# A graph attention layer on one core: edge values by four 64x64 products, the messages' weights through PSUM, the clip in two parts

## The chip, the core and the metric

The program runs on one core of one Trainium2 chip. The metric is device microseconds from launch to end; lower is better. Three runs of the kernel before gave 1743.85, 1745.33 and 1745.64 us.

## The reference

A layer of graph attention over N = 6250 nodes of 64 values (4 heads of 16) and 206250 edges, sorted by destination, and then a sum with x and a layer norm of each node:

```python
Qh = (x @ Wq.T + bq).reshape(n, H, D)          # Kh, Vh alike
Ee = (edge_attr @ We.T + be).reshape(-1, H, D)
score = (Kh[src] * Qh[dst] * (1.0 / np.sqrt(D)) * Ee).sum(-1)
score = jnp.exp(jnp.clip(score, -5.0, 5.0))
msg = Vh[src] * score[..., None]
wV = jax.ops.segment_sum(msg, dst, num_segments=n)
x = _layernorm(x + wV.reshape(n, H * D), axis=-1)
```

## The kernel before

After a first part that makes tables of K, V and Q for all nodes, the edges are worked through in 202 groups g of 8 tiles of 128 edges. A loop over g holds one step of each stage of a software pipeline, and the order in which a step's instructions are written is the order in which each engine runs them. Waits between engines are set by the framework from what each instruction reads and writes.

The stages of one group, with the engine and the line of each:

- edges(g), on TensorE: the 64x64 matrix We times the edge attributes of 1024 edges, in f32. The attributes come as a tile of 128 partitions, where partitions 0 to 63 hold the 64 attributes of the even tiles of edges and partitions 64 to 127 those of the odd ones. We stands twice in a 128x128 matrix with zeros beside (we_sb), and one product of 128 by 512 fills the PSUM bank ee. It runs three groups ahead.
- biased(g), on ScalarE (L695): adds the bias, ee to eb in SBUF.
- queries(g), on TensorE: picks the rows of Q that the edges need, by a one-hot matrix. These are two products with 64 output rows each, one to partitions 0 to 63 and one to partitions 64 to 127 of the bank qq.
- terms(g), on VectorE (L708): eb times qq. turn(g), on TensorE (L713): four f32 transposes of the result into the bank qe.
- products(g), on VectorE: K of the sources times qe (L732), a sum over each head's 16 values (L735), and the clip to -5 and 5 (L737). weigh(g), on ScalarE (L741): the exponential, in place in SBUF. message(g), on VectorE (L753): V times the weight, into qe.
- keep and take (L765, L770), on ScalarE and VectorE: split the f32 message into three bf16 parts.
- sums(s), on TensorE: for a pair s of groups, 16 products of 192 columns that add the messages of each destination, into the 192 columns pa of the bank room. add(s), on VectorE (L805, L811): adds the three parts into sum_, the last 64 columns of the same bank, and then into the nodes' accumulators.

Beside this runs a second stream. Of every group some of the K and V rows aren't fetched from the table but picked on TensorE: VectorE makes one-hot blocks (hots, L644), five and then three or four blocks in a step, and for each block TensorE runs three products of 512 columns (picks, the tiles pick0 and pick1). These picks are the body of each step on TensorE. About every third group a batch of picks ends; then a product with the bias (bkv_p) and eight f32 products (w2, x) make K and V of it. The other K and V rows are gathered by GpSimd (L260), which issues each gather at a marked place in TensorE's order.

On TensorE a step is written as: edges(g+3), the picks (in every second step with four of the 16 sums after each two blocks but the first two), turn(g+1), queries(g+2), and the sums that are left. All of these products are recorded at one line, L684, so they are told apart by tile. On VectorE add(s) is written near the step's end, ahead of terms(g+2).

## Time and profile before

| | |
|---|---|
| median of three runs | 1745.33 us |
| the profiled execution | 1744.26 us |
| its span, first to last instruction | 1742.4 us |
| TensorE busy | 95% of the span |
| VectorE busy | 90% |
| GpSimd busy | 75% |
| ScalarE busy | 53% |
| granted TensorE clock, mean | 0.974 |

The span is what the trace covers; 1.9 us of the execution lie around it. Busy time says how long an engine had an instruction in work. Matmuls overlap each other in the records, so the length of one matmul's record is not what it costs TensorE: the cost is the time from its start to the start of the next one, called its slot below.

### The profile page before, as it was taken

Reading aid. Unit: us, or ns where it says so; the run is one execution under the profiler, and the core shown is the slowest. Engines: PE = TensorE matmul, PEld = TensorE weight load, DVE = VectorE, ACT = ScalarE, POOL = GpSimd, SP = SyncE. Lnnn points to the kernel's source line nnn. Section 1 sums busy time; section 2 is a strip of 40 time slices with the busy share of each in tenths; the row PEclk is TensorE's granted clock in tenths of the full one; section 3 lists DMA queues with packets and bytes.
Section 4 is the critical chain, followed back from the end, with each engine's and each line's share of the span. In section 5 each row is a group of like instructions: output and inputs, shape, how many; then the busy total and the mean of one; then the engine's idle time right before and its main releaser. Section 6 shows DMA issues by size and latency. Waiting matters only on the chain.

```text
span 1742.4 us, 26109 instructions
## 1 busy us (share of the span) xinstructions
PE 1661.7 (95%) x8456; PEld 881.2 (51%) x8611; DVE 1569.6 (90%) x2637; ACT 918.4 (53%) x1507; POOL 1310.5 (75%) x1374
## 2 busy tenths in 40 slices
PE   7779999999999999999999999999999999999964
PEld 6435555555555555555555555555555555555533
DVE  5689999999999999999999999999999999999976
ACT  3655555545555555555555555555555555555553
POOL 7777777777777777777777777777777777777775
PEclk9879999999999999999999999999999999999985
DMA  6744444343443443434434344344343443434331
GB/s 191 246 120 133 112 118 116 102 121 101 117 120 103 120 113 104 122 108 121 121 102 120 104 114 118 99 120 117 106 132 97 120 113 103 121 107 125 108 89 47
DMA packets 115144, 203.65 MB, mean 117 GB/s; under 512 B 55475, under 2 KB 56223, under 8 KB 114885
## 3 DMA queue, kind: packets, MB, share of 16 engines
q1 hardware_dynamic: 70914, 112.68, 21.7%
q0 software_dynamic: 43648, 88.17, 19.5%
q10 hardware_dynamic: 436, 1.04, 0.3%
q8 instruction: 69, 1.13, 0.3%
q14 instruction: 77, 0.63, 0.1%
HBM read 194.18 MB, written 7.59 MB: 116 GB/s over the span
## 4 chain that ended last, share of the span: by engine, by line
PE 90%; DMA 3%; DVE 2%; issue 2%; ACT 2%; POOL 1%; SPq 0%; POOLq 0%; DVEq 0%; ACTq 0%
PE pick L684 62%; PE ee L684 11%; PE room L684 7%; PE qe L713 5%; PE qq L684 4%; DMA kv<-kv_tab,src_i 2%; POOL kv L260 1%; PE ps L462 1%; DMA wkv<-in_wT 1%; DMA et<-in_eT 0%; PE pv L542 0%; DVE score L735 0%; DVE prod L732 0%; DVE term L708 0%; ACT eb L695 0%
## 5 line engine op out<-in xcount | busy, mean ns | idle before, releaser
L260 POOL DMA_INDIRECT kv<-kv_tab,src_i x1324 | 1270.7, 960 | 403.5 <-issue 197.1
L684 PE MATMUL pick<-hot,parts 128*128 128x512 bf16 x4495 | 1052.4, 379 | 8.3 <-issue 0.2
L684 PEld LDWEIGHTS <-parts 128*128 128x128 bf16 x4650 | 451.9, 98 | 527.1 <-issue 73.3
L644 DVE TENSOR_TENSOR hot<-from,still 128x2560 bf16<-128x2560 bf16 x366 | 460.0, 1257 | 0.0
L741 ACT ACTIVATE score<-score 128x32 f32<-128x32 f32 x202 | 46.3, 229 | 732.7 <-DVE score L737 732.7
L765 ACT ACTIVATE msg<-qe 128x512 bf16<-128x512 f32 x400 | 238.6, 596 | 35.8 <-DVE qe L753 26.9
L684 PE MATMUL ee<-et,we_sb 128*128 128x512 f32 x404 | 227.4, 645 | 7.1 <-ACT eb L695 6.1
L249 ACT ACTIVATE to<-to,one_p 126x1024 bf16<-126x1024 bf16 x198 | 226.5, 1144 | 0.0
L243 ACT ACTIVATE to<-kb,minus_row 126x1024 bf16<-126x1024 uint8 x198 | 224.6, 1134 | 0.0
L684 PE MATMUL room<-msg,of 128*128 128x192 bf16 x1592 | 200.2, 252 | 17.6 <-DVE y L811 11.3
L684 PEld LDWEIGHTS <-of 128*128 128x128 bf16 x1600 | 142.8, 100 | 109.5 <-DVE y L811 19.9
L770 DVE TENSOR_TENSOR msg<-qe,msg 128x512 bf16<-128x512 f32 x200 | 136.9, 685 | 67.4 <-ACT msg L765 61.3
L708 DVE TENSOR_TENSOR term<-eb,qq 128x512 f32<-128x512 f32 x202 | 137.0, 678 | 20.1 <-PE qq L684 15.8
L770 DVE TENSOR_TENSOR qe<-qe,msg 128x512 f32<-128x512 f32 x200 | 138.2, 691 | 18.2 <-ACT msg L765 18.2
L732 DVE TENSOR_TENSOR prod<-kv,qe 128x512 f32<-128x512 f32 x202 | 137.3, 680 | 8.2 <-DMA kv<-kv_tab,src_i 3.4
L735 DVE TENSOR_REDUCE score<-prod 128x32 f32<-128x512 f32 x202 | 138.3, 685 | 7.0
L713 PE MATMUL qe<-ident,term 128*128 128x128 f32 x806 | 126.2, 281 | 18.7 <-DVE term L708 18.7
L753 DVE TENSOR_TENSOR qe<-kv,score 128x512 f32<-128x512 f32 x200 | 139.0, 695 | 4.1 <-ACT score L741 4.1
L695 ACT ACTIVATE eb<-ee,be_col 128x512 f32<-128x512 f32 x202 | 135.1, 669 | 4.6 <-PE ee L684 4.6
L724 DVE TENSOR_TENSOR of<-still,key 128x2048 bf16<-128x2048 bf16 (+2 forms) x105 | 122.7, 1169 | 0.2
L713 PEld LDWEIGHTS qe<-ident,term 128*128 128x128 f32 x806 | 97.3, 144 | 49.8 <-DVE term L708 29.9
L684 PE MATMUL qq<-to,qw 126*64 126x512 bf16 x396 | 82.4, 413 | 0.0
(138 smaller groups left out, 855.5 us busy)
## 6 DMA issues: line engine op xcount, KB each, us to landing
et<-in_eT SPq DMA_DIRECT2D x100, 512.0 KB
kb<-key_tab SPq DMA_DIRECT2D x101, 252.0 KB
kv<-kv_tab,src_i POOLq DMA_INDIRECT x1324
srcs<-in_src_rows SPq DMA_DIRECT2D x62, 256.0 KB
qw<-q_tab SPq DMA_DIRECT2D x202, 15.8 KB
kv_tab<-kv_sb SPq DMA_DIRECT2D x4, 640.0 KB
q_tab<-q SPq DMA_DIRECT2D x5, 480.0 KB
y<-in_x_blocks SPq DMA_DIRECT2D x2, 512.0 KB
```

The lines of the kernel that those rows point to most:

```text
L243: nc.scalar.activation(TO[g][:, :n, :], KB.pop(g)[:, :n * P].rearrange("p (j e) -> p j e", j=n), AF.Square, bias=minus_row3[:3 * W])
L249: nc.scalar.activation(TO[g][:, :n, :], TO[g][:, :n, :], AF.Relu, bias=one_p[:3 * W], scale=-1.0)
L260: return nc.gpsimd.indirect_dma_start(out=kv_of(g)[:, j, :], out_offset=None, in_=kv_tab[:, :], in_offset=bass.IndirectOffsetOnAxis(ap=src ...
L644: nc.vector.tensor_tensor(HOT[k][:, :hi - lo].rearrange("p b (a c) -> p b a c", c=2), pairs(FROM[m])[:, None].to_broadcast(shape), block2[ ...
L684: mark.append(nc.tensor.matmul(*aps, **kw))
L708: nc.vector.tensor_mul(TERM[g][:, :n], EB.pop(g)[:, :n], qq[:, :n])
L713: nc.tensor.transpose(qe[g % 2][:, 2 * u:2 * u + 2, :].rearrange("p j c -> p (j c)"), TERM[g][:, u, :], ident)
L732: nc.vector.tensor_mul(prod[:, :n, :], kv_of(g)[:, :n, :C], qe[g % 2][:, :n, :])
L735: nc.vector.tensor_reduce(score, prod[:, :n, :].rearrange("p g (h d) -> p g h d", h=H), axis=AX.X, op=OP.add)
L753: nc.vector.tensor_mul(to.rearrange("p g (h d) -> p g h d", h=H), kv_of(g)[:, :n, C:].rearrange("p g (h d) -> p g h d", h=H), SCORE[g][:, ...
L765: nc.scalar.activation(part, left, AF.Copy)
L770: nc.vector.tensor_sub(left if i == 0 else part_of(g, 2)[1], left, part)
```

## The change

It has four parts.

1. The product of 128x128 by 512 becomes four products of 64x64 by 256 columns. Product (u, r) takes the attributes at partitions 64r to 64r+63 and the matrix We that stands at the same partitions, and writes partitions 64u to 64u+63 of bank r of the tile room, which now has two banks. The halves u are the first and the second half of the group's tiles of edges, so queries and turn index their tiles anew.
2. The tile room holds edge values in columns 0 to 255 of both banks. Bank 0 has pa and sum_ behind them, bank 1 the weights of three groups. The bank of ee is gone, and the count of banks stays at eight.
3. The clip at L737 goes. ScalarE computes relu(5 - score) and then exp(5 - that), which is exp(min(score, 5)), and writes this to PSUM. The message becomes one VectorE instruction that takes the maximum of the weight and exp(-5) and multiplies it with V.
4. The sums of a pair stand in one run of 16 at the end of the step, behind queries, and no more among the picks. add(s) is always written ahead of the picks' part of the step, so on VectorE it comes earlier.

```diff
-            room = fixed.tile([P, 4 * P], F32, name="room")
-            pa = room[:, :3 * C]
-            sum_ = room[:, 3 * C:4 * C]
+            room = fixed.tile([P, 2, 4 * P], F32, name="room")
+            ee = room[:, :, :2 * P].rearrange("p r (i e) -> p r i e", e=P)
+            pa = room[:, 0, 2 * P:2 * P + 3 * C]
+            sum_ = room[:, 0, 2 * P + 3 * C:2 * P + 4 * C]
+            weights = [room[:, 1, 2 * P + C + k * G * H:2 * P + C + (k + 1) * G * H]
+                       .rearrange("p (g h) -> p g h", g=G) for k in range(3)]
...
             def edges(g):
-                n = tiles_of(g) // 2
-                product(ee[:, :n, :], we_sb, ET[g][:, :n, :], start=True, stop=True)
+                n = tiles_of(g) // 4
+                for u in range(2):
+                    for r in range(2):
+                        rows = slice(r * C, (r + 1) * C)
+                        product(ee[u * C:(u + 1) * C, r, :n, :], we_sb[rows, rows],
+                                ET[g][rows, u * n:(u + 1) * n, :], start=True, stop=True)
...
-                nc.vector.tensor_scalar(score, score, -5.0, 5.0, op0=OP.max, op1=OP.min)
...
             def weigh(g):
-                score = SCORE[g][:, :tiles_of(g)]
-                nc.scalar.activation(score, score, AF.Exp)
+                n = tiles_of(g)
+                score = SCORE.pop(g)[:, :n]
+                nc.scalar.activation(score, score, AF.Relu, bias=five_p, scale=-1.0)
+                WEIGHT[g] = weights[g % 3][:, :n]
+                nc.scalar.activation(WEIGHT[g], score, AF.Exp, bias=five_p, scale=-1.0)
...
-                nc.vector.tensor_mul(to.rearrange("p g (h d) -> p g h d", h=H),
-                                     kv_of(g)[:, :n, C:].rearrange("p g (h d) -> p g h d", h=H),
-                                     SCORE[g][:, :n, :, None].to_broadcast([P, n, H, D]))
+                nc.vector.scalar_tensor_tensor(
+                    to.rearrange("p g (h d) -> p g h d", h=H),
+                    WEIGHT.pop(g)[:, :, :, None].to_broadcast([P, n, H, D]), LEAST,
+                    kv_of(g)[:, :n, C:].rearrange("p g (h d) -> p g h d", h=H),
+                    op0=OP.max, op1=OP.mult)
...
-                if g > groups_of(ONES - 1)[-1]:
-                    for s in done:
-                        add(s)
+                for s in done:
+                    add(s)
...
-                summed = 0
-                for i, some in enumerate(by_two(todo)):
+                for some in by_two(todo):
                     picks(some)
-                    if i and parted and g - 1 in ends:
-                        sums(ends[g - 1], summed, summed + 4)
-                        summed += 4
...
                 if g - 1 in ends and now:
-                    sums(ends[g - 1], summed)
+                    sums(ends[g - 1])
...
-                if g <= groups_of(ONES - 1)[-1]:
-                    for s in done:
-                        add(s)
```

How TensorE's order changes at the turn of one step to the next, half way through the program, in the kernel before (the last number of a row counts equal rows; the size is that of the output):

```order
L713 MATMUL qe_759<-ident,term 128x128 x4
L684 LDWEIGHTS qw
L684 MATMUL qq<-to,qw 64x512
L684 LDWEIGHTS qw
L684 MATMUL qq<-to,qw 64x512
L684 MATMUL ee<-et,we_sb 128x512
L684 LDWEIGHTS ones_b
L684 MATMUL pick_753<-bkv_p,ones_b 128x512
```

And at the same place of the kernel after, where lines are numbered anew:

```order
L727 MATMUL qe_760<-ident,term 128x2x64 x4
L691 LDWEIGHTS qw
L691 MATMUL qq<-to,qw 64x512
L691 LDWEIGHTS qw
L691 MATMUL qq<-to,qw 64x512
L691 MATMUL room<-et,we_sb 64x256 x4
L691 LDWEIGHTS ones_b
L691 MATMUL pick_755<-bkv_p,ones_b 128x512
```

One row for the edge values has become four, of half the rows and half the columns each, at the same place between the queries and the next step's products.

On ScalarE a step from its exponential on, before:

```order
L741 ACTIVATE score<-score 128x32
L695 ACTIVATE eb<-ee,be_col 128x512
L243 ACTIVATE to<-kb,minus_row_84 126x1024
L765 ACTIVATE msg<-qe_759 128x8x64
L249 ACTIVATE to<-to,one_p 126x1024
```

and after:

```order
L754 ACTIVATE score<-score,five_p 128x32
L756 ACTIVATE room<-score,five_p 128x32
L706 ACTIVATE eb<-room,be_col 128x2x2x128
L247 ACTIVATE to<-kb,minus_row_84 126x1024
L782 ACTIVATE msg<-qe_761 128x8x64
L253 ACTIVATE to<-to,one_p 126x1024
```

One instruction has come in ahead of the exponential, whose output is now in the tile room, and eb reads that same tile.

On VectorE a step with an add, from the reduction of the scores on, before:

```order
L735 TENSOR_REDUCE score<-prod 128x32
L737 TENSOR_SCALAR score<-score 128x32
L644 TENSOR_TENSOR hot<-from,still 128x2560
L753 TENSOR_TENSOR qe_760<-kv_67,score 128x512
L644 TENSOR_TENSOR hot<-from,still 128x2048
L770 TENSOR_TENSOR qe_760<-qe_760,msg 128x512
L724 TENSOR_TENSOR of<-still,key 128x2048
L770 TENSOR_TENSOR msg<-qe_760,msg 128x8x64
L805 TENSOR_REDUCE room<-room 128x64
L811 TENSOR_SCALAR y<-room,above,y 128x64
L811 TENSOR_SCALAR y<-room,below,y 128x64
L708 TENSOR_TENSOR term<-eb,qq 128x512
```

and after:

```order
L748 TENSOR_REDUCE score<-prod 128x32
L651 TENSOR_TENSOR hot<-from,still 128x2560
L768 TENSOR_SCALAR qe_761<-room,kv_67 128x512
L651 TENSOR_TENSOR hot<-from,still 128x2048
L787 TENSOR_TENSOR qe_761<-qe_761,msg 128x512
L822 TENSOR_REDUCE room<-room 128x64
L828 TENSOR_SCALAR y<-room,above,y 128x64
L828 TENSOR_SCALAR y<-room,below,y 128x64
L737 TENSOR_TENSOR of<-still,key 128x2048
L787 TENSOR_TENSOR msg<-qe_761,msg 128x8x64
L721 TENSOR_TENSOR term<-eb,qq 128x512
```

The clip is gone, the message reads the tile room, and the three instructions of add stand ahead of the one-hot block of the sums (the output named of) instead of behind it.

The framework keeps engines apart by whole PSUM banks. So in the built program the exponential waits for the four edge products of its step, the message waits for eb of its step, and edges(g+3) waits for the last add, the last eb and the last message, since these touch the two banks of room.

More of the change, by code (lines that the diff above doesn't have):

```diff
@@ L1 @@
+import math
 from contextlib import ExitStack
@@ L50 @@
 REST = N - BIG * P
+CLIP = 5.0
+LEAST = math.exp(-CLIP)
 def tiles_of(g):
@@ L602, in tile_gnn @@
                 tc.tile_pool(name="psum", bufs=1, space=bass.MemoryType.PSUM) as psum:
-            OH, OF, EB, TERM, MSG, SCORE, HOT = ({} for _ in range(7))
+            OH, OF, EB, TERM, MSG, SCORE, WEIGHT, HOT = ({} for _ in range(8))
             still = fixed.tile([P, 4 * P], F32, name="still")
@@ L694, in biased @@
                 EB[g] = work.tile([P, G // 2, P], F32, name="eb")
-                nc.scalar.activation(EB[g][:, :n], ee[:, :n], AF.Identity, bias=be_col)
+                nc.scalar.activation(EB[g][:, :n].rearrange("p (i r) e -> p r i e", r=2),
+                                     ee[:, :, :n // 2], AF.Identity, bias=be_col)
             def queries(g):
@@ L700, in queries @@
                 for u in range(2):
-                    product(qq[u * C:(u + 1) * C, :n // 2, :], QW[g], TO[g][:, u:n:2, :],
+                    product(qq[u * C:(u + 1) * C, :n // 2, :], QW[g],
+                                     TO[g][:, u * n // 2:(u + 1) * n // 2, :],
                                      start=True, stop=True)
@@ L710, in turn @@
             def turn(g):
-                for u in range(tiles_of(g) // 2):
-                    nc.tensor.transpose(qe[g % 2][:, 2 * u:2 * u + 2, :].rearrange("p j c -> p (j c)"),
-                                        TERM[g][:, u, :], ident)
+                half = tiles_of(g) // 2
+                for k in range(half):
+                    nc.tensor.transpose(qe[g % 2][:, k:k + half + 1:half, :], TERM[g][:, k, :], ident)
             def onehot_edges(s):
@@ L778, in pa_of, with sums @@
             def pa_of(s):
-                return {NS - 3: px[0][:, :3 * C], NS - 2: px[1][:, :C], NS - 1: ee[:, 0, :C]}.get(s, pa)
-            def sums(s, lo=0, hi=2 * G):
+                return {NS - 3: px[0][:, :3 * C], NS - 2: px[1][:, :C], NS - 1: room[:, 1, 2 * P:2 * P + C]}.get(s, pa)
+            def sums(s):
                 n = tiles_in(s)
-                for j in range(lo, min(hi, n)):
+                for j in range(n):
                     product(pa_of(s), (OF if s >= WHOLE else OH)[s][:, j, :],
```

3 lines of the change are left out of this document (2 added, 1 removed).

## The prediction, as it stood before the changed kernel was run

> **What bounds the kernel now.** I read the page's shares and chain first, then busy time by stage, then TensorE's waits, then its timeline over one step and a half.
>
> ```profile
> span 1742.4 us, 26109 instructions
> PE 1661.7 (95%) x8456; PEld 881.2 (51%) x8611; DVE 1569.6 (90%) x2637; ACT 918.4 (53%) x1507; POOL 1310.5 (75%) x1374
> PE 90%; DMA 3%; DVE 2%; issue 2%; ACT 2%; POOL 1%; SPq 0%; POOLq 0%; DVEq 0%; ACTq 0%
> ```
>
> ```profile
> 0.00:100.00 100.00, 71.37 (x227) 52.92 (x227) 61.76 (x173) 52.72 (x129) 73.78 (x85) 0.89 0.68 205
> 500.00:1000.00 500.00, 497.38 (x2593) 257.79 (x2642) 466.15 (x754) 265.75 (x423) 379.92 (x395) 1.00 0.41 113
> 1690.00:1742.40 52.40, 24.53 (x106) 16.69 (x104) 35.83 (x89) 20.61 (x35) 30.02 (x32) 0.57 0.19 48
> ```
>
> The columns of a stretch are its length, then busy time of PE, PEld, DVE, ACT and POOL. In the middle TensorE is busy 497 of 500 us at full clock; only the first 100 us and the last 52 leave it idle. What TensorE waited for from 100 to 1690 us is this:
>
> ```profile
> PE qe L713 <- DVE term L708: 11.0, 5, 4.6
> PE ee L684 <- ACT eb L695: 3.9, 3, 1.6
> PE pick L684 <- DVE x L666: 1.8, 1, 1.8
> ```
>
> Under 17 us in 1590, and 9 waits in all. So between 100 and 1690 us the time is the sum of TensorE's slots, and a change there counts in full, while VectorE, ScalarE and GpSimd have room. The number of groups in this stretch is that of the clips, 192:
>
> ```profile
> 100.00:1690.00 1590.00, 38.97 (x192) 0.99 0.41 114
> ```
>
> **What a slot costs.** TensorE's timeline over one step and its ends, and three answers of narrower windows that show single starts:
>
> ```profile
> 906.26 0.49 PE L684 MATMUL room<-msg,of 128*128 128x192 bf16 x4
> 906.59 0.60 PE L713 MATMUL qe<-ident,term 128*128 128x128 f32 x4
> 907.12 0.41 PE L684 MATMUL qq<-to,qw 126*64 126x512 bf16 x2
> 907.46 0.50 PE L684 MATMUL room<-msg,of 128*128 128x192 bf16 x4
> 907.80 1.05 PE L684 MATMUL ee<-et,we_sb 128*128 128x512 f32 x2
> 908.69 5.34 PE L684 MATMUL pick<-hot,parts 128*128 128x512 bf16 x24
> 913.87 0.60 PE L713 MATMUL qe<-ident,term 128*128 128x128 f32 x4
> 914.40 0.41 PE L684 MATMUL qq<-to,qw 126*64 126x512 bf16 x2
> 914.74 1.12 PE L684 MATMUL ee<-et,we_sb 128*128 128x512 f32 x2
> 915.70 0.81 PE L684 MATMUL pick<-hot,parts 128*128 128x512 bf16 x2
> ```
>
> ```profile
> 906.70 0.49 PE L713 MATMUL qe<-ident,term 128*128 128x128 f32 x3
> ```
>
> ```profile
> 908.26 0.59 PE L684 MATMUL ee<-et,we_sb 128*128 128x512 f32 x1
> ```
>
> ```profile
> 915.27 0.59 PE L684 MATMUL ee<-et,we_sb 128*128 128x512 f32 x1
> ```
>
> - A pick of 512 bf16 columns: (913.87 - 908.69) / 24 = 0.216 us. A product of sums: 0.33 / 4 = 0.082.
> - One f32 edge product is two matmuls, which I call passes. Each has a slot of 0.43 (915.27 to 915.70, and 908.26 to 908.69), twice a pick's.
> - The first pass's slot is 0.53 behind the queries (914.74 to 915.27) and 0.46 behind sums (907.80 to 908.26). The 0.10 over 0.43 is the loading of f32 weights that nothing hid; behind sums most of it was hidden.
> - The two queries use different halves of the array's columns and take 0.34 together (914.40 to 914.74), 0.12 more than one product of that length. So they run side by side.
> - A change of the array's shape costs: the last transpose ahead of the queries has 0.20 (four take 0.53, and 906.59 to 906.70 is one of 0.11), so 0.09 on the way in. On the way out it is the 0.12, of which 0.05 may be 64 columns of weights, so 0.07.
>
> A group's edge product thus costs 0.96 behind queries, 0.89 behind sums. By the order two of three stand behind queries: 0.94.
>
> **The change on TensorE.** It puts four products in place of one. Each has a quarter of the work and still two passes, 256 columns each: 0.215 (half of 0.43). That makes eight passes, 1.72 us of streaming, and the whole question is how many lie beside each other. The order of issue is first pass, second pass of product (0,0), then both of (0,1), (1,0), (1,1). Two rows bound it: the queries show that neighbours in different parts of the array overlap; the edge product's own passes show that a second pass doesn't start before the first has streamed. If issue is in order, as all starts in the timeline are, the second pass of a product holds up all behind it, and only the next product's first pass joins it. Eight passes then take five rounds, not two. Weights of 64 columns I estimate at 0.05, half of 0.10; the first is bare, and those of the next three products' first passes are issued behind the second pass ahead of them, another 0.05 each. With 0.08 for leaving the shape:
>
> 0.05 + 5 x 0.215 + 3 x 0.05 + 0.08 = 1.355 us, against 0.94: +0.415 us a group, x 192 = **+80 us**.
>
> Two smaller terms. In half the groups the four now stand behind 16 sums in the full array, so they pay 0.09 to enter: 96 x 0.09 = +9. The 62 groups with a bias product behind them paid for that product's own shape already, which the exit now covers:
>
> ```profile
> 898.06 1.12 PE L684 MATMUL ee<-et,we_sb 128*128 128x512 f32 x2
> 899.11 0.39 PE L684 MATMUL pick<-bkv_p,ones_b 3*128 3x512 bf16 x1
> ```
>
> There 1.05 stands for 0.96, so 62 x 0.09 = -6. Sum: +83 us. The ten other groups stand in the start and the tail, where TensorE idles: nothing.
>
> The unknown prices from both sides: if all later weights load hidden, -0.15 x 192 = -29; with loads of 0.10 instead of 0.05, four of them, +38.
>
> **The other engines.** One step without sums on VectorE and ScalarE:
>
> ```profile
> 907.57 0.69 DVE L708 TENSOR_TENSOR term<-eb,qq 128x512 f32<-128x512 f32 x1 [0.60 <-PE qq L684]
> 908.18 0.68 DVE L732 TENSOR_TENSOR prod<-kv,qe 128x512 f32<-128x512 f32 x1
> 908.89 0.69 DVE L735 TENSOR_REDUCE score<-prod 128x32 f32<-128x512 f32 x1
> 909.62 0.18 DVE L737 TENSOR_SCALAR score<-score 128x32 f32<-128x32 f32 x1
> 909.71 1.48 DVE L644 TENSOR_TENSOR hot<-from,still 128x2560 bf16<-128x2560 bf16 x1
> 911.11 0.69 DVE L753 TENSOR_TENSOR qe<-kv,score 128x512 f32<-128x512 f32 x1
> ```
>
> ```profile
> 909.83 0.23 ACT L741 ACTIVATE score<-score 128x32 f32<-128x32 f32 x1 [3.58 <-DVE score L737]
> 909.97 0.67 ACT L695 ACTIVATE eb<-ee,be_col 128x512 f32<-128x512 f32 x1
> ```
>
> Without the clip the one-hot block can start some 0.20 earlier: it stands 0.82 behind the reduction now (908.89 to 909.71), where two neighbours of that length stand 0.61 apart (907.57 to 908.18). The message with two operations isn't in the trace; the nearest row, the same kind on 128x512, takes 0.74 against 0.69 to 0.70:
>
> ```profile
> L666 DVE SCALAR_TENSOR_TENSOR x<-odd,upper,pick 128x512 f32<-128x512 int32 x61 | 44.9, 736 | 0.0
> L753 DVE TENSOR_TENSOR qe<-kv,score 128x512 f32<-128x512 f32 x200 | 139.0, 695 | 4.1 <-ACT score L741 4.1
> ```
>
> So VectorE gains 0.16 a group, worth nothing while TensorE sets the time. ScalarE gets 0.23 a group more, at 53% busy.
>
> New waits: the message now waits for eb as well, since both touch one bank. The reduction ends at 909.58, and ScalarE follows VectorE by 0.03 (the clip ends at 909.80): relu 909.61 to 909.84, exponential 909.87 to 910.10, eb 910.13 to 910.80. The one-hot block of 1.48, from 909.5, covers this. In steps that follow sums, 16 of them from 907.46 end at 908.77, and the four products 1.45 later at 910.22. The exponential waits for them, 0.35 past its 909.87, and the message starts at 911.2 and not 910.9: 0.3 us on VectorE in every second step. Behind the message wait the second one-hot block, the splitting and the terms, which TensorE needs a step later; the 34 us of every 500 that VectorE idles cover it. If that cover went (a TensorE faster than VectorE), it would cost 96 x 0.3 = 29 us. The sums in one run keep their 16 slots of 0.082; add stands earlier, so that the next edges don't wait for it: nothing. The gathers hang on places in TensorE's order and move with it.
>
> **The Trainium skill on this.** "TensorE: Matmul & The Clock Gate", Part 3, section "The mechanism", says that matmuls start and end strictly in program order; by that rule the sum is the 1.355 above, and every start in the timeline agrees. Against it stands "TensorEngine Tiling (Array Packing)", section "Key Properties": tiles work independently, and different ones load and multiply in parallel. By this rule alone the eight passes are two rounds, the first rival's time; the queries agree for one pass each, and no run here shows it for two.
>
> **Rivals.**
> - All four side by side (faster). If a second pass waits at its own part of the array and lets the next product past, a group costs 0.05 + 2 x 0.215 + 0.08 = 0.56: -0.38 x 192 + 3 = -70 us, 1674; with 0.3 us of VectorE's new wait laid bare in part, up to 1700. For it: the queries' overlap. Against it: the second edge pass is never recorded ahead of the first one's end. It decides below four rounds of 0.215: four with their loads cost about as much as today's 0.94.
> - Halves. If only products on the same rows queue behind each other, there are three rounds: 0.05 + 0.645 + 0.05 + 0.08 = 0.825, -0.115 x 192 + 3 = -19 us: 1725.
> - It doesn't do what it says: f32 passes don't overlap at all. Eight rounds and 0.13: 1.85, +0.91 x 192 + 3 = +178 us, 1922. Against it the queries speak, though those are bf16.
>
> **How the numbers follow.** The profiled execution took 1744.26 us, 1.1 below the median shown; 1744 + 83 = **1827 us**. The likeliest case's own range, by the bounds of weights, is 1790 to 1868. Chances: in order 0.60, side by side 0.22, halves 0.07, no overlap 0.07, else 0.04. The range reaches down to side by side and leaves out the 1922: 1674 to 1868. About 0.2% is what a measurement of this kernel can tell from none. Faster by more than that: 0.22 + 0.07 + 0.01 = 0.30; within it 0.03; slower 0.60 + 0.07 = 0.67.
>
> **What would show it.** In the timeline after, the slot from the first edge matmul to whatever follows the four: 1.3 to 1.4 with six or so distinct starts says in order; 0.6 says side by side; 1.8 says no overlap. The picks must keep 0.216 and TensorE 99% busy in the middle; a TensorE that idles for VectorE would prove the cover wrong. VectorE's busy share should fall in the slower cases only because the span grows. I am wrong if the records show second passes starting ahead of the first one's end.

## The result and the profile after

The kernel after took 1728.72 us, the median of four runs from 1727.84 to 1729.15; the kernel before 1744.92. The ratio is 0.9906, with a 95% interval from 0.9894 to 0.9919: 16 us faster, where 83 us slower was forecast.

The page and the stretches of the kernel after, in the views that were shown of before:

```profile
span 1726.9 us, 28900 instructions
PE 1605.5 (93%) x9637; PEld 860.0 (50%) x9823; DVE 1547.7 (90%) x2436; ACT 994.1 (58%) x1709; POOL 1293.2 (75%) x1374
PE 60%; DVE 14%; DMA 8%; ACT 8%; issue 6%; POOL 2%; DVEq 0%; POOLq 0%; SPq 0%; ACTq 0%
```

```profile
0.00:100.00 100.00, 69.06 (x269) 52.63 (x269) 60.29 (x169) 53.99 (x131) 72.91 (x84) 0.86 0.67 205
500.00:1000.00 500.00, 488.75 (x3007) 255.35 (x3066) 470.31 (x710) 292.06 (x490) 378.11 (x401) 1.00 0.42 114
1690.00:1726.90 36.90, 15.04 (x76) 11.24 (x73) 19.90 (x49) 8.66 (x18) 17.75 (x19) 0.55 0.18 45
```

TensorE had 90% of the chain that ended last and has 60% now. VectorE, ScalarE and the gathers' DMAs share 30%. In the middle TensorE idles 11 of 500 us, where it idled under 3. Its waits from 100 to 1690 us:

```profile
PE room L691 <- DVE y L828: 24.8, 17, 6.3
PE room L691 <- DVE acc L828: 10.3, 4, 4.7
PE room L691 <- DVE qe L768: 10.2, 6, 2.5
PE room L691 <- ACT msg L782: 8.0, 3, 4.0
PE qe L727 <- DVE term L721: 3.2, 3, 1.1
```

So 56 us of waits stand where the kernel before had 17, and nearly all of them are of the tile room, in which edge values, sums and weights now live together. TensorE's timeline at the place that the prediction quoted, with an answer of a window that ends 0.04 us behind the first edge product:

```profile
899.30 0.41 PE L691 MATMUL qq<-to,qw 126*64 126x512 bf16 x2
899.64 0.66 PE L691 MATMUL room<-et,we_sb 64*64 64x256 f32 x8
900.23 6.00 PE L691 MATMUL pick<-hot,parts 128*128 128x512 bf16 x26
908.36 0.66 PE L691 MATMUL room<-et,we_sb 64*64 64x256 f32 x8
908.96 0.38 PE L691 MATMUL pick<-bkv_p,ones_b 3*128 3x512 bf16 x1
```

```profile
899.64 0.45 PE L691 MATMUL room<-et,we_sb 64*64 64x256 f32 x4
```

All eight passes have a slot of 0.59 to 0.60 us together (899.64 to 900.23, 908.36 to 908.96), not 1.355. The second answer shows how: four of the eight start at 899.64. In the trace's records they start at 899.636, .643, .649 and .656, and the other four at 899.903, .909, .916 and .923. That is two rounds. If first and second pass of each product are issued one behind the other, as the prediction had it, the second pass of (0,0) waited at its own part of the array and let three products past. The records don't name the product that a pass belongs to; e7 below shows that products do pass each other.

Where TensorE's time went is a sum of slots. I added the time from each matmul's start to the next one's, by tile, from the use of group 12's gathered rows to that of group 186's (174 groups), in us. f1 and k2 are runs of the next section.

| tiles | before | after | f1 | k2 |
|---|---|---|---|---|
| edge products | 168.7 | 104.5 | 103.5 | 103.5 |
| queries | 58.7 | 84.1 | 80.8 | 65.3 |
| sums, picks, batches | 1130.2 | 1140.4 | 1141.9 | 1140.8 |
| transposes | 92.2 | 92.2 | 92.2 | 92.2 |
| the stretch | 1449.8 | 1421.3 | 1418.2 | 1401.8 |

The edge products gave 64 us. Of these, 25 came back in the slots of the queries: the edge products stand behind the queries in half the steps, and their wait for room is counted in the slot ahead of them (22 us; the other 4 are sums that wait for room). Another 10 came back in sums, picks and batches: the last sum's slot ahead of the small products is 0.176, where it was 0.082, as forecast, in 87 of the steps (8 us). So the stretch is 28.5 us shorter; the start and the tail then took 13 us more (what lies behind group 186 is 133.5 us, 123.1 before). This is the second half of the riddle: what made the tail longer, and what TensorE waits for.

### The profile page after: what moved, and what is told of

The parts are those of the page before. It is cut to its first block, busy times and chain, and to the rows that moved or that the text cites. A ratio compares the mean times of both kernels' runs of the same rounds, so it can differ in the third digit from the quotient of the medians.

```text
span 1726.9 us, 28900 instructions
## 1 busy us (share of the span) xinstructions
PE 1605.5 (93%) x9637; PEld 860.0 (50%) x9823; DVE 1547.7 (90%) x2436; ACT 994.1 (58%) x1709; POOL 1293.2 (75%) x1374
## 4 chain that ended last, share of the span: by engine, by line
PE 60%; DVE 14%; DMA 8%; ACT 8%; issue 6%; POOL 2%; DVEq 0%; POOLq 0%; SPq 0%; ACTq 0%
PE pick L691 44%; PE room L691 10%; DMA kv<-kv_tab,src_i 7%; PE qe L727 3%; POOL kv L264 2%; PE qq L691 2%; DVE score L748 2%; ACT eb L706 2%; DVE prod L745 2%; DVE term L721 2%; DVE hot L651 2%; DVE qe L787 1%; DVE qe L768 1%; ACT msg L782 1%; ACT to L253 1%
## 5 line engine op out<-in xcount | busy, mean ns | idle before, releaser
L264 POOL DMA_INDIRECT kv<-kv_tab,src_i x1324 | 1253.4, 947 | 404.7 <-issue 192.6
L691 PE MATMUL pick<-hot,parts 128*128 128x512 bf16 x4464 | 1026.1, 381 | 10.2 <-issue 0.5
L691 PEld LDWEIGHTS <-parts 128*128 128x128 bf16 x4650 | 446.3, 98 | 559.3 <-issue 57.1
L754 ACT ACTIVATE score<-score,five_p 128x32 f32<-128x32 f32 x202 | 64.9, 321 | 661.1 <-DVE score L748 661.1
L691 PE MATMUL room<-msg,of 128*128 128x192 bf16 x1592 | 156.0, 253 | 34.0 <-DVE y L828 14.4
L691 PE MATMUL room<-et,we_sb 64*64 64x256 f32 (+1 forms) x1616 | 139.8, 417 | 37.5 <-DVE y L828 18.4
L768 DVE SCALAR_TENSOR_TENSOR qe<-room,kv 128x512 f32<-128x512 f32 x200 | 139.9, 700 | 31.5 <-ACT eb L706 23.8
L691 PEld LDWEIGHTS <-of 128*128 128x128 bf16 x1600 | 132.8, 100 | 59.6 <-issue 34.5
L706 ACT ACTIVATE eb<-room,be_col 128x512 f32<-128x512 f32 x202 | 138.7, 686 | 9.6 <-PE room L691 1.8
L737 DVE TENSOR_TENSOR of<-still,key 128x2048 bf16<-128x2048 bf16 (+2 forms) x105 | 123.0, 1172 | 0.2
L691 PEld LDWEIGHTS room<-et,we_sb 64*64 64x64 f32 x1616 | 44.0, 136 | 79.1 <-issue 33.0
```

What stands on the lines that cost most here:

```text
L264: return nc.gpsimd.indirect_dma_start(out=kv_of(g)[:, j, :], out_offset=None, in_=kv_tab[:, :], in_offset=bass.IndirectOffsetOnAxis(ap=src ...
L691: mark.append(nc.tensor.matmul(*aps, **kw))
L706: nc.scalar.activation(EB[g][:, :n].rearrange("p (i r) e -> p r i e", r=2), ee[:, :, :n // 2], AF.Identity, bias=be_col)
```

## The experiments

Four theories were tried. A: the gain is lost where edges and sums wait for room. B: VectorE is full. C: the message waits for eb, since ScalarE's new operations stand ahead of it on one tile. D: GpSimd's gathers are a stream that is full, and they end the program. All kernels are the kernel after with an edit, if nothing else is said.

**e1_four_alone** takes the weights out of PSUM again, with the clip of before; the four products and the new order stay.

```diff
+                nc.vector.tensor_scalar(score, score, -5.0, 5.0, op0=OP.max, op1=OP.min)
...
-                nc.scalar.activation(score, score, AF.Relu, bias=five_p, scale=-1.0)
-                WEIGHT[g] = weights[g % 3][:, :n]
-                nc.scalar.activation(WEIGHT[g], score, AF.Exp, bias=five_p, scale=-1.0)
+                nc.scalar.activation(score, score, AF.Exp)
...
+                nc.vector.tensor_mul(to.rearrange("p g (h d) -> p g h d", h=H),
```

> The kernel after with only its first, second and fourth part: four edge products in the shared tile room, but the clip on VectorE, the exponential in SBUF and the message as before. Theory A (TensorE's edge slot fell by 0.34 us a group, 62 us between 120 and 1640 us, and about two thirds came back as waits of the edges for add and of the sums for the message, plus some 8 us in the tail): the message no longer reads room, so the sums wait less, but VectorE has the clip again, 0.2 us a group; 1725 to 1740 us, edge slot 0.60. Rival B (VectorE, 94% busy in the middle, is simply full, and any saving beyond its time is lost): the clip's 0.16 us a group comes on top of the 1729 in full, +31: 1755 or more, no gain over the kernel before. Rival C (the new path of the weights, with the message waiting for eb, costs what was lost): 1690 to 1705.

1740.07 us, 0.9978 (0.9969 to 0.9988). Four products without the weights' path bring 4 of the 16 us. Why the weights help was open at this point; e4 answers it.

**e2_full_array** keeps all but the four products: two products of the full array, 256 columns each.

```diff
-                for u in range(2):
-                    for r in range(2):
-                        rows = slice(r * C, (r + 1) * C)
-                        product(ee[u * C:(u + 1) * C, r, :n, :], we_sb[rows, rows],
-                                ET[g][rows, u * n:(u + 1) * n, :], start=True, stop=True)
+                for r in range(2):
+                    product(ee[:, r, :n, :], we_sb, ET[g][:, r * n:(r + 1) * n, :], start=True, stop=True)
```

> The kernel after, but the edge values by two products in the full 128x128 array, 256 columns each, into the same two banks; all else stays. Four passes of 0.215 with weights loaded twice: an edge slot of 0.95 to 1.1 in place of 0.60. Theory A: TensorE gets 0.35 to 0.5 us a group longer, 67 to 96 us, and the waits for add and message fall by some 30: 1765 to 1795. Rival B (VectorE sets the time): under 1750, since TensorE's 62 us were not what counted. Rival C: like A, less nothing: 1790 or more.

1754.39 us, 1.0063 (1.0047 to 1.008), in none of the three ranges. In its middle TensorE is full again:

```profile
500.00:1000.00 500.00, 496.22 (x2708) 280.90 (x2756) 460.31 (x693) 287.36 (x484) 377.94 (x401) 1.00 0.41 114
```

```profile
903.41 1.13 PE L691 MATMUL room<-et,we_sb 128*128 128x256 f32 x4
904.47 0.39 PE L691 MATMUL pick<-bkv_p,ones_b 3*128 3x512 bf16 x1
```

A slot of 1.06 against 0.60. So the 64x64 products do give the time, 26 us between this kernel and the one after, and the rest of the change costs 9 us by itself.

**e3_add_early** writes add(s) directly behind the products, against the waits for add.

```diff
                     weigh(g)
+                for s in done:
+                    add(s)
...
-                for s in done:
-                    add(s)
```

> The kernel after with add(s) written directly behind the scores' reduction, ahead of the one-hot blocks and the message, so that VectorE does it some 4 us earlier in its step. Theory A: the edges' waits for add, 24 us between 120 and 1640 us, go; VectorE gets no work less. 1700 to 1715, TensorE's waits for add below 6 us. Rival B: the time lost moves to another wait of TensorE for VectorE, 1724 to 1732. Rival C: 1724 to 1732.

1784.89 us, 1.0233 (1.0216 to 1.025): a miss. The waits moved into the chain of every second step, as its waits from 100 to 1690 us show:

```profile
ACT eb L706 <- DVE y L828: 79.3, 79, 1.0
DVE room L822 <- ACT room L756: 66.9, 94, 0.7
```

The second line says that add's first operation, on bank 0, waits for the exponential into bank 1. So the framework keeps engines apart by the whole tile of two banks, not by single banks as the section on the change has it.

**e4_weights_sbuf** lets the exponential write to SBUF, so that the message waits no more for eb.

```diff
-                WEIGHT[g] = weights[g % 3][:, :n]
+                WEIGHT[g] = work.tile([P, G, H], F32, name="weight", bufs=3)[:, :n]
```

> The kernel after with the exponential's output in SBUF in place of room's second bank; relu, exponential and the two-operation message stay. So the message waits for the exponential alone and not for eb, and the exponential not for the edge products. Theory A: VectorE loses 24 us of idle time ahead of the message, so add comes earlier and the edges wait less: 1710 to 1722. Rival B: the same by 24 us less of VectorE's time, 1705 to 1715. Rival C: all of the lost 46 us come back, 1680 to 1690. If it is 1727 or more, the wait for eb was covered, as the prediction had it.

1746.03 us, 1.001 (1.0 to 1.002): a miss again, and the one that led to the gathers. GpSimd's groups over the whole program, before, after and e4 in this order (one line of each; behind the bar busy us, mean ns, idle time):

```profile
L260 POOL DMA_INDIRECT kv<-kv_tab,src_i x1324 | 1270.7, 960 | 403.5 <-issue 197.1 <-PE pick L684 65.9 <-DMA kv<-kv_tab,src_i 48.8
```

```profile
L264 POOL DMA_INDIRECT kv<-kv_tab,src_i x1324 | 1253.4, 947 | 404.7 <-issue 192.6
```

```profile
L264 POOL DMA_INDIRECT kv<-kv_tab,src_i x1324 | 1271.6, 960 | 404.1 <-issue 186.8 <-PE pick L691 89.6 <-DMA kv<-kv_tab,src_i 42.4
```

The idle time is 0.30 us ahead of each of 1324 gathers, the same in all three kernels, whoever is named as its releaser. So the gathers follow each other without a break, and 75% busy is a full stream. Its ends, the first and the last gather, in the kernel after and then in the kernel before:

```profile
55.44 0.97 POOL L264 DMA_INDIRECT kv<-kv_tab,src_i  x1 [0.30 <-issue]
...
1712.29 0.95 POOL L264 DMA_INDIRECT kv<-kv_tab,src_i  x1 [0.30 <-issue]
```

```profile
55.60 0.94 POOL L260 DMA_INDIRECT kv<-kv_tab,src_i  x1 [0.30 <-issue]
...
1728.53 0.94 POOL L260 DMA_INDIRECT kv<-kv_tab,src_i  x1 [0.30 <-issue]
```

(1712.29 - 55.44) / 1323 = 1.252 us for each in the kernel after, and 1.2645 in the kernel before. 16 us lie between the two last gathers, as much as the whole gain. Behind its last gather a kernel needs 13.9 us (before) or 14.6 to 14.9 (after, e1, e4) to its end; in e2 and e3, where the gathers are done early, it is 33 to 35. So the gathers ended the kernel before as well. In e4 VectorE waits for the rows from 900 to 1300 us, as it does not before:

```profile
DVE prod L745 <- DMA kv<-kv_tab,src_i: 11.1, 8, 2.5
```

The lead of a group (the time from its last gather's issue to the use of its rows; 2.5 to 3 is as short as it gets), mean of 7 groups from g on, in us:

| g | before | after | e1 | e4 | e2 |
|---|---|---|---|---|---|
| 33 | 30.4 | 30.4 | 29.3 | 26.4 | 37.3 |
| 103 | 24.4 | 16.2 | 12.5 | 3.7 | 38.6 |
| 173 | 16.1 | 4.4 | 4.1 | 3.6 | 39.6 |
| 194 | 9.3 | 4.5 | 2.8 | 3.2 | 32.0 |

The kernel after has little of its lead left from about group 173 on, e4 from 103. The kernel before has 3.0 and 3.1 left at its last two groups.

Why a gather is 13 ns longer in e4: I counted, over gathers 6 to 1260, those above 1.0 us that overlap the message (the VectorE instruction that multiplies V by the weight) in time.

| kernel | the message's inputs | overlaps | above 1.0 us | mean gather |
|---|---|---|---|---|
| before | both in SBUF | 240 | 63 | 960 ns |
| e1 | both in SBUF | 238 | 55 | 955 ns |
| e4 | both in SBUF | 247 | 62 | 959 ns |
| after | weight in PSUM | 256 | 0 | 946 ns |

Taken together, the gathers above 1.0 us exceed 0.945 by 19.8 us in the kernel before, by 18.3 in e4 and by 2.5 in the kernel after. That accounts for the 16 us. Since e4's edit moves nothing but the weights, their place is what makes the gathers longer. An instance in the kernel before:

```profile
902.86 0.69 DVE L753 TENSOR_TENSOR qe<-kv,score 128x512 f32<-128x512 f32 x1
903.21 1.16 POOL L260 DMA_INDIRECT kv<-kv_tab,src_i  x1 [0.30 <-issue]
```

The Trainium skill names such a conflict: "GPSIMD Engine Reference", section "Specifications", says that GpSimd's way to SBUF is shared with VectorE and contended by VectorE instructions with two SBUF inputs. The rows agree for the message, and for the one-hot blocks, which have one input in PSUM (the tile still): of 596 overlaps in the kernel after none is above 1.0 us. Of the 15 longer gathers that are left there, 14 lie beside odd<-srcs (L234), a VectorE instruction with a single int32 input in SBUF.

**e5 to e8** ran under conditions in which the kernel before itself took 2050.93 us, with stalls of about a microsecond on TensorE for which the profile names nothing; they stand against each other at most. The edits: e5 means to write the edge products behind the first two blocks of picks, but its condition leaves out the step in which a batch ends and the two behind it, and a batch ends in every third step: only the steps of groups 6 and 7 change. e6 gives the two banks to two tiles, with the bias in two parts; e7 makes eight products of 128 columns; e8 is the kernel before with the change's order alone.

```diff
+                picked_now = by_two(todo)
+                if picked_now and g not in READY and g - 1 not in READY and g - 2 not in READY:
+                    picks(picked_now.pop(0))
                 if g + 3 < NG:
```

```diff
-            room = fixed.tile([P, 2, 4 * P], F32, name="room")
+            room = fixed.tile([P, 4 * P], F32, name="room")
+            hall = fixed.tile([P, 4 * P], F32, name="hall")
```

```diff
-                        product(ee[u * C:(u + 1) * C, r, :n, :], we_sb[rows, rows],
+                        for i in range(n):
+                            product(ee[u * C:(u + 1) * C, r, i, :], we_sb[rows, rows],
```

```diff
-                    if i and parted and g - 1 in ends:
-                        sums(ends[g - 1], summed, summed + 4)
-                        summed += 4
```

> The kernel after with edges(g+3) written behind the first two blocks of picks of its step (six products, 1.3 us) instead of ahead of them, in the steps where no batch of picks begins or ends its way to K and V. Theory A (the gain is lost where the edges wait for add, since both touch the tile room): the wait for add, 24 us between 120 and 1640 us in pieces of 0.3 to 2.7, is covered up to 1.3 us each; about 5 of it is left: 1708 to 1716 us. Rival B (VectorE is as good as full, and TensorE waits for it elsewhere if not there): 1724 to 1732. A loss, 1735 or more, would say that the exponential, which waits for the edges, is what can't be late.

> The kernel after with room's two banks as two tiles, so that only what touches the same bank waits for each other; the bias is added by two instructions of 256, the bank of the weights first. The message then waits for the second bank's half of eb, the sums no more for message and exponential; ScalarE gets some 0.25 us a group more. Theory A: VectorE's idle time ahead of the message (24 us) and the sums' wait for the message (8 us) shrink, the edges' wait for add stays: 1716 to 1724. Rival B: 1720 to 1727, as VectorE's work stays. If ScalarE's work counts: 1732 or more.

> The kernel after with each of the four edge products cut into two of 128 columns, issued one behind the other, so that each part of the array has four passes in a row and not two. If a part of the array can hold several passes in waiting, the edge slot stays at 0.60 to 0.70 us: 1729 to 1745. If it holds only one, the third pass holds up the other parts, the slot is 1.0 or more: 1775 to 1815. The prediction's reasoning (no pass waits at its part) would have it above 1.3.

> The kernel before with the fourth part alone: the 16 sums in one run behind the queries, and add always ahead of the step's picks. Theory A and rival B: TensorE sets the time, the sums keep their slots and nothing new waits: 1742 to 1747 us. If the new order itself costs (sums that wait for the message's parts, VectorE's work bunched): 1750 or more, and part of what the kernel after lost is the order's.

They gave 2071.18, 2073.29, 2096.05 and 2050.22 us. e7's trace answers one thing regardless: sixteen passes of 128 columns have a slot of 0.62, so their count costs little and the streaming decides.

```profile
908.47 0.69 PE L691 MATMUL room<-et,we_sb 64*64 64x128 f32 x16
909.09 6.07 PE L691 MATMUL pick<-hot,parts 128*128 128x512 bf16 x27
```

Its starts also say how the passes are issued. Here each part of the array has two products, four passes, in a row in the program. Still the first four starts lie 13 ns apart (908.473, .486, .500 and .513), and the next four come from 908.633 on. So the products of three other parts started ahead of the second product of (0,0), which is written before them. From one part to the next it is 3 ns in the two queries (one pass each), 6.7 in the kernel after (two passes each) and 13 here (four): 3.3 ns a pass, as if each pass is issued in the program's order and waits at its own part.

**f1_fewer_gathers** tests D: the kernel after without one gather in seven from group 10 on, 1132 instead of 1324. The K and V of those edges stay an older group's.

```diff
         (g, js), after = lot
+        if g >= 10 and js == [3]:
+            return
```

> The kernel after, without the gather of tile 3 of each group from group 10 on: that tile's K and V are those of an older group, so the values are not the layer's; all other work stays. GpSimd has some 1132 gathers to issue and not 1324. Theory D, new: the kernel after ends when GpSimd's gathers do (1324 at 1.251 us from 55 us on, without a pause, then 15 us), and TensorE's and VectorE's own pace would end only a little earlier, since TensorE also waits for add: 1710 to 1720 us, most of the gain from group 173 on, where the gathers had come within 3 us of their use. Theory A alone (all was lost in the waits at room): 1727 to 1731. Rival B (VectorE full): 1727 to 1731.

1717.56 us, 0.9843 (0.9827 to 0.986), as D has it. The gathers held 11 us. What lies behind group 186 fell from 133.5 to 126.6 us.

**f2_fewer_later** is f1 with e5's edit, **f3_edges_later** is e5 again.

> As the run with fewer gathers (the same gather is left out, the values are not the layer's), and the edges of each step stand behind the first two blocks of picks, so that the wait for add is covered up to 1.3 us. Theory D with A (two limits close together: the gathers, and behind them TensorE's waits for add): 1690 to 1702. D with B (behind the gathers stands VectorE's own work): no better than with fewer gathers alone, 1710 to 1720.

> The kernel after with the edges of each step behind the first two blocks of picks, all gathers in place: the kernel that ran on the chip with a slow TensorE before. Theory D: GpSimd's stream is full already, so nothing is to be had: 1725 to 1731, with the gathers' lead used up earlier than group 173. Theory A alone: 1708 to 1716. Rival B: 1724 to 1732, but with the lead used up no earlier.

1716.2 us (0.9837, 0.9821 to 0.9853) and 1727.87 us (0.9902, 0.9886 to 0.9919), the times of f1 and of the kernel after. They say nothing on A: in f3's trace the edge products stand behind picks twice, at 120.8 and 129.5 us, and behind queries or sums nearly everywhere else, as without the edit. Whether edges that stand later, or in a tile of their own, would lose less was not tested.

**f4_fewer_sbuf** is f1 with e4's edit.

> The kernel with the weights in SBUF (1746 us, 17 more than the kernel after), without the same one gather in eight (the values are not the layer's). Theory D: the message with both inputs in SBUF cost time only by holding up gathers that lie beside it (1.265 us a gather against 1.251), so without the gathers as limit the 17 us go: within 5 us of the run with fewer gathers and the weights in PSUM. If the weights in SBUF cost VectorE or ScalarE something of their own: 10 us or more above that run.

1703.3 us, 0.9764 (0.9747 to 0.978), below anything expected. With the gathers out of the way, weights in SBUF are 14 us faster than weights in PSUM; with all gathers they were 17 slower. Both limits are real, and the change's third part trades one for the other.

**h1 to h4** met the same conditions as e5 to e8 (the kernel before at 2050.69). h1 writes ScalarE's bias ahead of the step's products and weights, h2 is this with f1's edit, h3 is h1 with one batch of picks more, h4 the kernel before with f1's edit.

```diff
                     edges(g + 3)
+                if g + 3 < NG:
+                    biased(g + 3)
                 if now:
...
                     weigh(g)
-                if g + 3 < NG:
-                    biased(g + 3)
```

```diff
-LAST = max(m for m in range(1, NG) if when(UNITS * m - 1) + 8 < NG)
+LAST = max(m for m in range(1, NG) if when(UNITS * m - 1) + 7 < NG)
```

> The kernel after with the bias of a step's edges (eb) ahead of relu and exponential on ScalarE, not behind them, so that eb is done while VectorE still reduces the scores, and the message waits for the exponential alone. Theory D (the gathers' stream is the limit of the kernel after): 1722 to 1728, almost nothing. If the message's wait for eb set the time: 1705 to 1715.

> The same order, without the gather of tile 3 of each group from group 10 on (the values are not the layer's). The gathers are no limit here, so the pace behind them shows. If the message's wait for eb is what made weights in PSUM 14 us slower than weights in SBUF with fewer gathers (1717 against 1703): 1699 to 1708. If it is something else that the shared tile room makes wait: 1712 to 1720.

> The same order with all of the layer's work, and one more batch of four K and V tiles picked on TensorE near the end, where it idles: 63 batches and not 62, so four gathers fewer. Theory D: 4 x 1.25 = 5 us off the limit, 1718 to 1724. If the end is set by TensorE or VectorE: 1727 to 1740, as the batch is 18 us of TensorE's time.

> The kernel before without the gather of tile 3 of each group from group 10 on (the values are not the layer's). If TensorE set the time of the kernel before from group 6 to group 192, as the prediction had it, only the tail of eight groups can gain, where the gathers' lead was used up: 1736 to 1744. If the gathers set it all along: 1700 to 1715.

2070.64, 1816.06, 2067.37 and 1792.22 us. Under these conditions the missing gathers take 255 to 258 us off either kernel; why TensorE's stalls go with them was not found, and nothing is concluded from them. h2 and h4 were run again as k2 and k1.

**k1_before_fewer** is h4's kernel, **k2_bias_first_fewer** is h2's.

> The kernel before without the gather of one tile in eight from group 10 on (that tile's K and V stay what was in the buffer, so the messages of those edges aren't the layer's). If TensorE alone held the kernel before: within 5 us of it, 1739 to 1746, with its lead of 20 us or more at every group. If the gathers held its last quarter: 1725 to 1735. The difference to the kernel after without the same gathers (1717.6) is then what the change brings with the gathers out of the way: 8 to 28 us.

> The kernel after without the same gathers, and with ScalarE's bias written ahead of the step's products and of the weights, so that eb no longer stands between the weights and the message. If the order on ScalarE makes the waits (C): 1700 to 1708 against 1717.6, and TensorE's waits of the edge products for add fall below 10 us. If VectorE's load or the shared tile makes them (A, B): within 4 us of 1717.6, waits as they were, 15 to 19 us.

k1: 1742.39 us, 0.9987 (0.9977 to 0.9996). The kernel before loses 2.5 us without the gathers. So TensorE's own order takes 1742.4 us and held the kernel up to its end, as the prediction read it; but the gathers' stream stood just above, and it set about the last 2.5 us. The kernel before was at two limits at once.

k2: 1692.37 us, 0.9692 (0.9676 to 0.9709), 25 us below f1 and more than C asked for. The stretch from 120 to 1600 us of f1 and k2, and in each the wait of room for add:

```profile
120.00:1600.00 1480.00, 1449.71 (x8890) 757.91 (x9069) 1391.39 (x2088) 870.70 (x1463) 983.51 (x1041) 1.00 0.39 110
```

```profile
PE room L693 <- DVE y L830: 16.4, 14, 2.1
```

```profile
120.00:1600.00 1480.00, 1473.98 (x9178) 766.27 (x9176) 1382.79 (x2111) 903.95 (x1478) 986.99 (x1045) 1.00 0.39 110
```

```profile
PE room L693 <- DVE y L830: 6.0, 7, 1.3
```

TensorE's idle time falls from 30 to 6 us with nothing changed on TensorE. Where it comes from is to be seen on VectorE and ScalarE, the kernel after first, then k2:

```profile
910.14 0.69 DVE L748 TENSOR_REDUCE score<-prod 128x32 f32<-128x512 f32 x1
910.75 1.48 DVE L651 TENSOR_TENSOR hot<-from,still 128x2560 bf16<-128x2560 bf16 x1
910.86 0.32 ACT L754 ACTIVATE score<-score,five_p 128x32 f32<-128x32 f32 x1 [2.20 <-DVE score L748]
911.22 0.29 ACT L756 ACTIVATE room<-score,five_p 128x32 f32<-128x32 f32 x1
911.54 0.69 ACT L706 ACTIVATE eb<-room,be_col 128x512 f32<-128x512 f32 x1
...
912.26 0.70 DVE L768 SCALAR_TENSOR_TENSOR qe<-room,kv 128x512 f32<-128x512 f32 x1
```

```profile
908.73 0.69 ACT L708 ACTIVATE eb<-room,be_col 128x512 f32<-128x512 f32 x1 [2.78 <-DVE term L723]
909.27 0.69 DVE L750 TENSOR_REDUCE score<-prod 128x32 f32<-128x512 f32 x1
909.87 1.48 DVE L653 TENSOR_TENSOR hot<-from,still 128x2560 bf16<-128x2560 bf16 x1
...
911.27 0.69 DVE L770 SCALAR_TENSOR_TENSOR qe<-room,kv 128x512 f32<-128x512 f32 x1
```

In the kernel after eb ends at 911.54 + 0.69 = 912.23 and the message starts 0.03 behind it. The one-hot block ends at 912.23 too (910.75 + 1.48), and so the wait can't be seen as idle time. But in k2 the message starts at 911.27, 0.08 ahead of the block's end (911.35), as VectorE's neighbours do where nothing is waited for. From the reduction's end to the message's start, mean over groups 20 to 185, it is 1.456 us in the kernel after and in f1, and 1.324 in k2. In some 190 groups the 0.13 us would be 25 us, f1 minus k2, but that they agree is chance: f4's message starts as early (1.325), and f4 is 14 us below f1.

The new order does one thing more. ScalarE's first split (msg<-qe) starts 0.04 us behind the message's end in k2, but 0.21 behind it in f1 and 0.23 in f4, where eb stands ahead of it. From the reduction's end to the start of VectorE's last subtraction of the step (msg<-qe,msg) it is 5.36 us in f1, 5.23 in f4 and 5.16 in k2; from one step's reduction to the next's 8.16, 8.10 and 8.06. So 14 of the 25 us are what it is worth that the message doesn't wait for eb: f4 takes the weights out of eb's tile. The other 11 go with the earlier split, most likely; it was not run alone.

What k2 says of A: the slots of the queries, with the waits for room in them, fall from 80.8 us in f1 to 65.3 with the tile and TensorE's order as they were. So most of these waits are for a VectorE that comes late, and it comes late by what it waits for on ScalarE.

## Why the prediction was wrong

- **"If issue is in order ... the second pass of a product holds up all behind it."** This step failed. The slot is 0.60 and not 1.355, two rounds and not five, and the largest term was not +80 but, over 174 groups, -64 (the first rival's -0.38 x 174 is -66). The rows that the step rested on showed passes of one product in one part of the array; they could not say what other parts do meanwhile. Of the two rules weighed, that of the Trainium skill's "TensorEngine Tiling (Array Packing)", section "Key Properties", holds here for two passes each. That of the Trainium skill's "TensorE: Matmul & The Clock Gate", Part 3, section "The mechanism", does not hold here: in e7 the products of three other parts are recorded ahead of one that is written before them.
- **The time of the rival that came true was too low as well.** It gave 1674, or up to 1700 with VectorE's new wait; 1728.7 was measured. That this lies inside the stated 1674 to 1868, and 4 us from the 1725 of the rival "Halves", is luck: that rival's slot is 0.825. (The likeliest case's own bounds give 1798 to 1865, not 1790 to 1868.) The statements behind the 1674 that failed are the next three.
- **"VectorE, ScalarE and GpSimd have room"** and "the gathers hang on places in TensorE's order and move with it". GpSimd's 75% is a stream without breaks: 55.4 + 1323 x 1.252 + 14.6 for the last group's way to the end = 1726.9, the span. In the kernel before the same sum, 55.6 + 1323 x 1.2645 + 13.9, is its span of 1742.4 too, 2.5 us above TensorE's own time (k1), and so it could hardly be seen as a wait. Whatever a faster TensorE gained beyond 2.5 us had to come from the gathers. Taking gathers out gave 11 us (f1). The 12 ns by which the gathers' pace got shorter, 16 us in 1323, are what let the end move down to here; that effect of the third part was not forecast.
- **"The one-hot block of 1.48, from 909.5, covers this."** The cover was short by 0.13 us a group. The prediction had relu at 0.23 and the exponential at 0.23, with eb done 1.22 behind the reduction's end; they take 0.32 and 0.29, and eb is done 1.40 behind it (912.23 - 910.83), when the block is just done. The condition was named, "a TensorE faster than VectorE", and its price too, 29 us; taking the wait away gave 14 (f4), or 25 together with the earlier split (k2). It comes in each group, though, not by 0.3 in every second one.
- **"Add stands earlier, so that the next edges don't wait for it: nothing."** TensorE waited 35 us for add (24.8 + 10.3), since the edges now share its tile and VectorE comes late.
- **"VectorE gains 0.16 a group, worth nothing."** The message takes 0.70, not the 0.74 of the nearest row, so the gain is 0.20. Whether it is worth something now wasn't measured apart. By f4, 0.13 a group on VectorE's chain is worth 14 us once TensorE's products are short and the gathers fewer.
- **Right:** TensorE bound the kernel before up to its last 2.5 us (k1); the picks keep their slots of 0.216; the small products pay 0.09 to be entered from sums; what would show the steps wrong was named, second passes against first ones and a TensorE that idles for VectorE, and both are there.

The ledger, in spans: the products' -64 becomes -54 with the way in (+10), -28.5 with the waits for room (+25), and -15.5 with the start and the tail (+13). Of the tail's 10 us the gathers hold 7 (f1). What stays open: k2's order with all its gathers was run only under the conditions of h1, where it can't be read. By the floor of the gathers it should end near the kernel after. Nor was A tested by itself, or the earlier split.

## What to carry to other kernels

For each engine that issues a stream, work out the slot from start to start times the count, and the lead of its transfers over the program: GpSimd's 0.30 us between gathers make a full stream look 75% busy, and a lead that shrinks from 30 to 16 us, and to 3 at the end, says that a second limit is near. A cover that is as long as what it hides to within 0.1 us is no cover: look how neighbours overlap where nothing is waited for, and compare starts. When the binding engine gets faster by 4%, the two next limits have to be priced with the same care as the gain.

## What was not expected of the hardware

- Eight f32 passes on four parts of the array run in two rounds: four starts 7 ns apart, the next four 0.25 us behind them. Sixteen run in four rounds with starts 13 ns apart (e7). A pass waits only at its own part.
- A gather beside a VectorE instruction with two f32 inputs in SBUF takes over 1.0 us in 63 of 240 cases, and in none of 256 where one input is in PSUM. Over 1324 gathers this is 13 ns each in the mean.
- On 128x32, ScalarE's relu and exponential with a bias from SBUF take 0.32 us each when they write to SBUF (e4) and the exponential 0.29 when it writes to PSUM, where the plain exponential took 0.23.
